# Attention score rows by way of DRAM lines, the last group graph by graph, and an urgent branch, in a four-layer graph network

## The chip, the cores and the metric

The kernel runs on one core of a Trainium2 chip. Its time is the device time of one execution in microseconds (us). Runs are compared by the median of several executions; one further execution was taken by the hardware profiler, and all views of the trace come from it. The engines are named as the profile names them: PE is TensorE (PEld its weight loads), DVE is VectorE, ACT is ScalarE, POOL is GpSimd, and SP is SyncE, which here issues DMAs. ACTq, DVEq and the like are the engines' own instruction queues. In the kernel's plan SP and ACTQ are the two queues for DMAs.

## What is computed

There are 128 graphs of 128 nodes with 256 features, and an adjacency matrix per graph. Four layers follow, each of the form x = x + f(relu(layernorm(x)), adj). All is float32.

```python
def _L0_gnn_ref(x, adj, weight, w_ih, w_hh, b_ih, b_hh):
    A = (adj != 0).astype(x.dtype)
    h = x
    for i in range(3):
        m = jnp.einsum('bnd,de->bne', h, weight[i])
        aggr = jnp.einsum('bst,bsd->btd', A, m)
        h = _gru_cell(aggr, h, w_ih, w_hh, b_ih, b_hh)
    return h

def _L1_gnn_ref(x, adj, relation, weight, bias):
    rel_ids = jnp.arange(1, weight.shape[0] + 1)
    masks = (relation[None] == rel_ids[:, None, None, None]).astype(x.dtype)
    h = jnp.einsum('rbnm,bmd->rbnd', masks, x)
    return jnp.einsum('rbnd,rdo->bno', h, weight) + bias

def _L2_gnn_ref(h, adj_mask, W, a):      # layer 3 is of the same kind
    Wh = jnp.einsum('bnd,od->bno', h, W)
    ei, ej = Wh @ a[:256], Wh @ a[256:]
    e = ei[:, :, None] + ej[:, None, :]
    e = jnp.where(e > 0, e, 0.2 * e)
    e = jnp.where(adj_mask == 0, -jnp.inf, e)
    alpha = jax.nn.softmax(e, axis=-1)
    return jnp.einsum('bij,bjo->bio', alpha, Wh)
```

For the change, the score matrix of the two attention layers matters: entry (i, j) is the sum of a number of node i, `ei`, and a number of node j, `ej`. With node i on the partitions, `ei` is a bias for each partition, but `ej` has to lie along the free axis, alike on all partitions. The first relational layer needs only one relation where the adjacency holds nothing but 0 and 1, as it does in these inputs; the kernel looks at the data to find that out.

## The kernel before, in words

The 128 graphs are handled in 32 groups of four (`G = 4`, `NG = 32`). For every group, `group(gi)` writes down operations: the loads (`load`, four DMAs on SP), a norm, three GRU steps (`step`, nearly all of the products, line 820), then the relational layer (`neighbours`), two attention layers (`attention` and `attend`) and the output (line 1096, on SP).

Nothing of the order is written by hand. Each operation is an `Op` with an engine, an estimated duration, and the buffers it reads and writes (whole or in parts). `Plan.order` then plays these durations through: it ranks each operation by the length of the way that hangs on it, moved by `PERIOD` (28 us) for each later group, and places again and again the operation that can start first; operations of up to `AHEAD = 4` groups mix. `LAG` and `HOP` are the allowances for a result to reach another engine (2500 ns for a DMA's landing), `OWN` for a result used on the same engine. The buffers (8 PSUM banks, 27 `big`, 10 `small`, 5 `xs` and others) are given out in this play too. The engines run the resulting lists strictly in order, with semaphores between them: an operation that has to wait on the chip holds everything behind it on its engine.

**The branch.** The operations up to the GRU steps are the same whatever the adjacency holds; later ones depend on it. The adjacency is therefore scanned: 32 loads on SP (line 508) and 32 maximum reductions on VectorE (L510), then one reduction (L513), a transpose on TensorE (L515), another reduction (L517) and a comparison into `found` (L519). All operations planned to start by then are issued; then all engines read `found` and branch (`values_load`, line 1111, and `tc.If`). In one side are all remaining operations with `neighbours`, in the other those with `relations`, which does not run here.

**Norm.** `norm` takes statistics for each graph (L532), then for each piece (a range of graphs) five small VectorE operations (L546 to L562) and a power on GpSimd (L558). Then ScalarE scales and shifts, two graphs in one operation (L574).

**Attention.** `attention(i, mask)` takes, for each graph, the sums for `ei` and `ej` (`terms`, L993) into columns of the tile `s`. `attend` then works on a piece. `rows` (L1018) transposes each column of `ej`, broadcast to 128 columns, on TensorE, so that a PSUM bank holds the row on all partitions. ScalarE adds `ei` as it copies the bank to the tile `e` (L1023). VectorE takes the leaky part (L1027), adds the mask and takes the minimum (L1030), ScalarE the exponential (L1036), VectorE the reciprocal (L1042, L1045). TensorE turns the weights round (L1054), they are evicted (L330, the line of all evictions that may run on ScalarE or VectorE), and for each pair of graphs come the weighted sum of nodes (L1065), an eviction, the product with the layer's weights (L1078) and the residual (L1088). In `neighbours`, L624 and L639 are the like products and L647 the residual.

A piece is the whole group (`whole`) for groups 0 to 28, and two graphs for the last three (`SPLIT = 3`).

Of the kernel before, what the change touches and what calls it, by code (L numbers as in the profile page):

```python
# [37 lines left out]
OWN = {"PE": 0, "ACT": 125, "DVE": 125, "POOL": 80, "SP": 0, "ACTQ": 0}  # L38
PERIOD = 28000
AHEAD = 4  # L40
SPLIT = 3
SPARE = (1, 0, 0, 3)
# [35 lines left out]
class Op:  # L78
    __slots__ = ("engs", "eng", "times", "ns", "fn", "deps", "heirs", "bufs", "group", "key", "port", "rank", "wait", "ready", "end")
# [12 lines left out]
class Plan:  # L92
# [6 lines left out]
    def op(self, eng, ns, fn, r=(), w=(), after=(), port=None):  # L99

        o = Op(*((eng, ns) if isinstance(eng, tuple) else ((eng,), (ns,))), fn, self.group)
        o.port = eng == "POOL" if port is None else port
        if self.shared:
            o.key = self.keys
            self.keys += 1
        deps = set(after)
        for items, writes in ((r, False), (w, True)):
            for item in items:  # L110
                buf, parts = item if isinstance(item, tuple) else (item, None)
                for other, wrote, theirs in buf.uses:
                    if buf.alone and o.engs + other.engs != ("PE", "PE"):
                        deps.add(other)
                    elif (writes or wrote) and other is not o:
                        if parts is None or theirs is None or parts & theirs:
                            deps.add(other)
                buf.uses.append((o, writes, parts))
                if buf not in o.bufs:
                    o.bufs.append(buf)  # L120
                    buf.left += 1
        o.deps = sorted(deps, key=lambda d: d.wait)
        o.wait = len(self.ops)
        for d in deps:
            d.heirs.append(o)
        self.ops.append(o)
        return o

    def order(self, pools, cut=None, prefix=()):
# [8 lines left out]
        for o in self.ops:  # L138
            o.rank = o.group * PERIOD - o.rank
            o.wait = len(o.deps)  # L140
# [112 lines left out]
def kernel(  # L253
# [40 lines left out]
    pools = [banks, xs, adjs, big, wide, half, small, mis]  # L294
# [3 lines left out]
    def build(general):  # L298
# [38 lines left out]
        def chunk(name):  # L337
            return Buf(big, name)
# [167 lines left out]
        for f in range(F):  # L506
# [7 lines left out]
            top.t[:, 0:1], most.t, AX.X, ALU.max), r=[most], w=[top])  # L514
        op("PE", 109, lambda: nc.tensor.transpose(pm.t[0:1, 0:P], top.t[:, 0:1], ident.t),  # L515
           r=[top, ident], w=[pm])
        op("DVE", 200, lambda: nc.vector.tensor_reduce(  # L517
            top.t[0:1, 1:2], pm.t[0:1, 0:P], AX.X, ALU.max), r=[pm], w=[top])
        verdict = op("DVE", 80, lambda: nc.vector.tensor_scalar(  # L519
            found, top.t[0:1, 1:2], 1.0, None, ALU.is_gt), r=[top])  # L520
# [5 lines left out]
        whole = (range(G),)  # L526

        def norm(xt, nm, pieces=whole):
# [39 lines left out]
            hs = []  # L568
            for g2 in range(G // 2):
                h = chunk(f"h{nm}{g2}")  # L570

                def scale(g2=g2, h=h):
                    for g in (2 * g2, 2 * g2 + 1):
                        nc.scalar.activation(  # L574
                            h.t[:, (g % 2) * D : (g % 2 + 1) * D], xt.t[:, g, :], AF.Relu,
# [3 lines left out]
                op("ACT", 2 * act(D, 2) + 85, scale,  # L579
                   r=[(xt, {2 * g2, 2 * g2 + 1}), (s, {(n, g) for n in ("rs", "mr") for g in (2 * g2, 2 * g2 + 1)})], w=[h])  # L580
                hs.append(h)
# [16 lines left out]
        def bias(xt):  # L598
            for g2 in range(G // 2):
                op("POOL", 1370, lambda g2=g2: nc.gpsimd.tensor_tensor(  # L600
                    xt.t[:, 2 * g2 : 2 * g2 + 2, :], xt.t[:, 2 * g2 : 2 * g2 + 2, :],
                    b1s.t.unsqueeze(1).to_broadcast([P, 2, D]), ALU.add),
                   r=[b1s], w=[(xt, {2 * g2, 2 * g2 + 1})])
# [7 lines left out]
        def neighbours(gi, xt, ai, aiT, m0, m3, late, pieces):  # L611
# [4 lines left out]
            hs, _ = norm(xt, f"1_{gi}", pieces)  # L616
            bias(xt)
            for g2 in range(G // 2):
                pr = bank(f"pr{gi}{g2}")

                def gather(g2=g2, pr=pr):
                    for g in range(2):
                        for k in range(KC):
                            nc.tensor.matmul(  # L624
                                pr.t[:, (2 * k + g) * P : (2 * k + g + 1) * P],
                                hs[g2].t[:, g * D + k * P : g * D + (k + 1) * P],
                                mT.t[:, (2 * g2 + g) * P : (2 * g2 + g + 1) * P],
                                start=True, stop=True,
                            )

                op("PE", 892, gather, r=[hs[g2], mT], w=[pr])
                hr = chunk(f"hr{gi}{g2}")
                evict(T, lambda hr=hr: hr.t, lambda pr=pr: pr.t, r=[pr], w=[hr])
                py = bank(f"py{gi}{g2}")

                def mix(hr=hr, py=py):
                    for g in range(2):
                        for k in range(KC):
                            nc.tensor.matmul(  # L639
                                py.t[:, g * D : (g + 1) * D],  # L640
                                hr.t[:, (2 * k + g) * P : (2 * k + g + 1) * P],
                                w1s.t[:, k, :],
                                start=(k == 0), stop=(k == KC - 1),
                            )

                op("PE", 2 * KC * 2 * D * PE_COL, mix, r=[hr, w1s], w=[py])
                op("DVE", dve(T), lambda g2=g2, py=py: nc.vector.tensor_tensor(  # L647
                    xt.t[:, 2 * g2 : 2 * g2 + 2, :], xt.t[:, 2 * g2 : 2 * g2 + 2, :],
                    py.t.rearrange("p (g d) -> p g d", g=2), ALU.add),
                   r=[py], w=[(xt, {2 * g2, 2 * g2 + 1})])  # L650

        def relations(gi, xt, ai, aiT, m0, m3, late, pieces):
# [55 lines left out]
        def group(gi):  # L708
# [272 lines left out]
            pieces = (range(2), range(2, G)) if gi >= NG - SPLIT else whole  # L981
            (relations if general else neighbours)(gi, xt, ai, aiT, m0, m3, late, pieces)
            unrelated(m2, m0, FAR, late)

            def attention(i, mask):
                hs, s = norm(xt, f"{2 + i}_{gi}", pieces)

                EI, EJ = 48, 52
                for g in range(G):
# [9 lines left out]
                    op("DVE", 690, terms, r=[hs[g // 2], ub[i]], w=[junk, (s, {("ei", g)})], port=True)  # L999
# [3 lines left out]
            def attend(i, mask, hs, s, gs, EI, EJ):  # L1003
# [9 lines left out]
                pe, e = bank(f"pe{nm}"), chunk(f"e{nm}")  # L1013
# [7 lines left out]
                op("PE", 110 * len(gs), rows, r=[ident, (s, {("ei", g) for g in gs})], w=[pe])  # L1021
                for g in gs:
                    op("ACT", 250, lambda g=g: nc.scalar.activation(  # L1023
                        at(e, g), at(pe, g), AF.Identity, bias=s.t[:, EI + g : EI + g + 1]),
                       r=[pe, (s, {("ei", g)})], w=[(e, {g})])
# [33 lines left out]
                for g2 in range(gs.start // 2, gs.stop // 2):  # L1059
                    pc, c, po = bank(f"pc{nm}{g2}"), chunk(f"cT{nm}{g2}"), bank(f"po{nm}{g2}")  # L1060

                    def weigh(g2=g2, pc=pc):
                        for g in range(2):
                            for k in range(KC):
                                nc.tensor.matmul(  # L1065
                                    pc.t[:, (2 * k + g) * P : (2 * k + g + 1) * P],
                                    hs[g2].t[:, g * D + k * P : g * D + (k + 1) * P],
                                    at(eT, 2 * g2 + g),
                                    start=True, stop=True,
                                )  # L1070

                    op("PE", 892, weigh, r=[hs[g2], eT], w=[pc])
                    evict(T, lambda c=c: c.t, lambda pc=pc: pc.t, r=[pc], w=[c])

                    def transform(c=c, po=po):
                        for g in range(2):
                            for k in range(KC):
                                nc.tensor.matmul(  # L1078
                                    po.t[:, g * D : (g + 1) * D],
                                    c.t[:, (2 * k + g) * P : (2 * k + g + 1) * P],  # L1080
                                    wa[i].t[:, k, :],
                                    start=(k == 0), stop=(k == KC - 1),
                                )

                    op("PE", 2 * KC * 2 * D * PE_COL, transform, r=[c, wa[i]], w=[po])
                    for g in range(2):
                        gg = 2 * g2 + g
                        op("DVE", 395, lambda g=g, gg=gg, po=po: nc.vector.scalar_tensor_tensor(  # L1088
                            xt.t[:, gg, :], po.t[:, g * D : (g + 1) * D], s.t[:, RI + gg : RI + gg + 1],
                            xt.t[:, gg, :], ALU.mult, ALU.add),  # L1090
                           r=[po, (s, {("rinv", gg)})], w=[(xt, {gg})])
# [69 lines left out]
```

## Time and profile before

| what | value |
|---|---|
| median of 3 runs | 2648.02 us (2647.67 to 2648.6) |
| the profiled execution | 2648.33 us |
| its span in the profile | 2646.5 us |
| TensorE transposes L1018 | 256, in sets of 4, 2 or 1 |
| ScalarE L1023, L1036 | 256 each, medians 373 and 394 ns |
| first start of the scan's loads, last of the scan's reductions | 21.3 us, 103.1 us |
| `found` written (L519) | 225.1 us |
| last residual L1088 begins to run | 2640.8 us |
| last output issued | 2641.7 us |
| granted TensorE clock, whole span | 0.994 |

The page lists busy times of the engines, the granted clock in slices of the span, and the chain of work that ended last, followed back from the last instruction. The other views are busy times by stretch, waits by releaser, and DMAs from issue to landing. Times within the trace count from the span's start.

### The profile page before, as it was taken

To read this page: it belongs to the slowest core of one execution; us is meant where nothing else is said; L and a number is where in the kernel's file an instruction comes from. 1 tells how busy PE (TensorE), PEld (TensorE's weight loads), DVE (VectorE), ACT (ScalarE), POOL (GpSimd) and SP (SyncE) were. 2 spreads that over 40 slices of the span, in tenths; PEclk is the share of its full clock that TensorE was granted. 3 is DMA by queue.
4 is the path that set the end of the run, shared out by engine and by line. 5 is a ranking of instruction groups with operands and counts; after the bars stand their busy time and mean duration, and the time that the engine had idled before them with its cause. 6 is when DMAs were issued, how large, how long until landed. Compare 5 with 4: busy or idle time off the path is not lost.

```text
span 2646.5 us, 40354 instructions
## 1 busy us (share of the span) xinstructions
PE 2606.2 (98%) x14041; PEld 2321.0 (88%) x14041; DVE 2204.8 (83%) x6376; ACT 1566.5 (59%) x3792; POOL 466.0 (18%) x400
## 2 busy tenths in 40 slices
PE   8999999999999999999999999999999999999995
PEld 7888888888888888988898988888888889888884
DVE  8868898888888888888888888888888888888885
ACT  5446666656566565565565656565656655665553
POOL 1112122111121111121111111111111111211121
PEclk9999999999999999999999999999999999999997
DMA  6100000000000000000000000000000000000000
GB/s 208 42 1 1 29 21 25 25 25 25 10 16 25 25 25 25 1 25 25 25 25 25 1 25 25 25 25 21 5 25 25 25 25 2 24 25 25 9 9 18
DMA packets 77494, 65.22 MB, mean 25 GB/s; under 512 B 3936, under 2 KB 73184, under 8 KB 77280
## 3 DMA queue, kind: packets, MB, share of 16 engines
q1 hardware_dynamic: 76192, 61.50, 7.8%
q8 instruction: 112, 1.84, 0.3%
q10 hardware_dynamic: 1088, 1.05, 0.1%
q14 instruction: 102, 0.84, 0.1%
HBM read 45.75 MB, written 16.78 MB: 24 GB/s over the span
## 4 chain that ended last, share of the span: by engine, by line
PE 94%; DVE 4%; ACT 1%; issue 0%; DMA 0%; POOL 0%; ACTq 0%; DVEq 0%
PE bank L820 64%; PE bank L1078 8%; PE bank L1065 4%; PE bank L762 4%; PE bank L639 4%; PE bank L954 3%; PE bank L733 2%; PE bank L624 2%; PE bank L1054 1%; PE bank L1018 1%; DVE junk L993 0%; PE bank L445 0%; DVE small L532 0%; DVE big L922 0%; DVE big L942 0%
## 5 line engine op out<-in xcount | busy, mean ns | idle before, releaser
L330 ACT COPY big<-bank 128x512 f32<-128x512 f32 (+1 forms) x978 | 455.5, 481 | 496.7 <-PE bank L820 426.3
L820 PE MATMUL bank<-big,rz_h 128*128 128x256 f32 x1536 | 462.8, 383 | 0.3
L820 PE MATMUL bank<-big,rz_a 128*128 128x256 f32 x1536 | 456.8, 379 | 0.0
L929 POOL TENSOR_TENSOR big<-wide,big 128x512 f32<-128x512 f32 x192 | 245.6, 1298 | 1108.7 <-ACT big L927 951.6
L820 PE MATMUL bank<-wide,rz_h 128*128 128x256 f32 x1152 | 342.9, 379 | 0.3 <-DVE wide L330 0.3
L820 PE MATMUL bank<-wide,rz_a 128*128 128x256 f32 x1152 | 342.6, 379 | 0.0
L820 PEld LDWEIGHTS bank<-big,rz_a 128*128 128x128 f32 x1536 | 291.8, 190 | 39.8
L820 PEld LDWEIGHTS bank<-big,rz_h 128*128 128x128 f32 x1536 | 279.7, 190 | 47.3 <-ACT big L330 15.0
L558 POOL TENSOR_TENSOR small<-small,nhalf 128x4 f32<-128x4 f32 (+1 forms) x137 | 138.8, 1014 | 970.4 <-DVE small L556 951.6
L574 ACT ACTIVATE big<-xs,small 128x256 f32<-128x256 f32 x512 | 269.8, 592 | 48.4 <-DVE small L562 48.0
L837 ACT ACTIVATE big<-big,b_rz 128x256 f32<-128x256 f32 x576 | 258.2, 499 | 44.3 <-DVE big L843 42.1
L330 DVE COPY big<-bank 128x512 f32<-128x512 f32 (+1 forms) x276 | 159.9, 581 | 143.8 <-PE bank L820 89.3
L927 ACT ACTIVATE big<-big,bih_s 128x512 f32<-128x512 f32 x192 | 128.7, 715 | 205.4 <-DVE big L912 109.1
L820 PEld LDWEIGHTS bank<-wide,rz_a 128*128 128x128 f32 x1152 | 218.9, 190 | 29.7
L820 PEld LDWEIGHTS bank<-wide,rz_h 128*128 128x128 f32 x1152 | 216.3, 190 | 28.5 <-DVE wide L330 0.5
L1078 PE MATMUL bank<-wa,big 128*128 128x256 f32 x1024 | 235.5, 383 | 2.6 <-ACT big L330 2.6
L843 DVE TENSOR_TENSOR big<-bank,big 128x512 f32<-128x512 f32 x288 | 196.2, 686 | 47.3 <-PE bank L820 46.8
L820 PE MATMUL bank<-big,n_h 128*128 128x256 f32 x768 | 228.2, 380 | 0.8 <-DVE big L330 0.7
L1078 PEld LDWEIGHTS bank<-wa,big 128*128 128x128 f32 x1024 | 195.0, 191 | 30.6 <-ACT big L330 4.2
L820 PE MATMUL bank<-big,n_a 128*128 128x256 f32 x768 | 217.9, 379 | 0.0
L912 DVE TENSOR_TENSOR big<-bank,big 128x256 f32<-128x256 f32 x384 | 160.6, 419 | 61.6 <-PE bank L820 57.9
L993 DVE CUSTOM_DVE_ANT_0 junk<-big,ub 128x256 f32<-128x256 f32 x512 | 192.6, 421 | 1.6 <-ACT big L574 1.5
(91 smaller groups left out, 4723.0 us busy)
## 6 DMA issues: line engine op xcount, KB each, us to landing
xs<-in_x_dram SPq DMA_DIRECT2D x64, 256.0 KB, 4.0
out_dram<-xs SPq DMA_DIRECT2D x29, 512.0 KB, 3.3
adjs<-in_adj_dram SPq DMA_DIRECT2D x32, 256.0 KB, 4.3
adjs<-in_adjT_dram SPq DMA_DIRECT2D x32, 256.0 KB, 4.5
big<-in_adj_dram SPq DMA_DIRECT2D x32, 256.0 KB, 3.0
out_dram<-xs SPq DMA_DIRECT2D x6, 256.0 KB, 2.2
big<-in_wihT_dram ACTq DMA_DIRECT2D x3, 256.0 KB, 6.4
big<-in_whhT_dram SPq DMA_DIRECT2D x3, 256.0 KB, 5.8
```

The costliest lines, as they stand in the source:

```text
L330: (nc.scalar.copy if eng == "ACT" else nc.vector.tensor_copy)(dst(), src())
L558: op("POOL", 1130, lambda: nc.gpsimd.tensor_tensor(columns(RS), columns(RS), nhalf.t[:, gs.start : gs.stop], ALU.pow), r=[nhalf], w=[own(" ...
L574: nc.scalar.activation(h.t[:, (g % 2) * D : (g % 2 + 1) * D], xt.t[:, g, :], AF.Relu, bias=s.t[:, MR + g : MR + g + 1], scale=s.t[:, RS + ...
L639: nc.tensor.matmul(py.t[:, g * D : (g + 1) * D], hr.t[:, (2 * k + g) * P : (2 * k + g + 1) * P], w1s.t[:, k, :], start=(k == 0), stop=(k = ...
L820: nc.tensor.matmul(ps.t[:, m * W : (m + 1) * W], a.t[(slice(None), *row, j, slice(m * P, (m + 1) * P))], b[j](), start=(start and m == x = ...
L837: op("ACT", act(W, 1) + 40, lambda m=m, c=c: nc.scalar.activation(t[c].t[:, g2 * W : (g2 + 1) * W], src.t[:, m * W : (m + 1) * W], AF.Tanh ...
L843: op("DVE", dve(T), lambda: nc.vector.tensor_tensor(c.t, ps.t, c.t, ALU.add), r=[ps], w=[c])
L912: op("DVE", dve(W), lambda: nc.vector.tensor_tensor(dst(), ps.t[:, :W], dst(), ALU.add), r=[ps], w=[((ws if more else vs)[c], {g2})])
L927: op("ACT", act(T, 1) + 85, lambda nn=nn, c=c: nc.scalar.activation(nn.t, vs[c].t, AF.Tanh, bias=bi.t[:, 4 + c : 5 + c]), r=[vs[c], bi], w ...
L929: op("POOL", 1230, lambda qq=qq, nn=nn, c=c: nc.gpsimd.tensor_tensor(qq.t, hT.t[:, c, :], nn.t, ALU.subtract), r=[(hT, {(c, 0), (c, 1)}), ...
L993: nc.vector.tensor_tensor_reduce(out=junk.t[:, v * D : (v + 1) * D], in0=part, in1=ub[i].t[:, v, :], op0=ALU.mult, op1=ALU.add, scale=1.0, ...
L1078: nc.tensor.matmul(po.t[:, g * D : (g + 1) * D], c.t[:, (2 * k + g) * P : (2 * k + g + 1) * P], wa[i].t[:, k, :], start=(k == 0), stop=(k ...
```

## The change

Five things are changed.

1. In `attend`, where the piece is the whole group (`len(gs) == G`), the transposes are left out. SP stores the four `ej` columns of `s` into a DRAM tile `line` (four graphs by 128 nodes), then loads this line into `e` on all partitions. ScalarE's addition reads `e` and writes `e`. There are four such lines, given out by the planner. Smaller pieces keep the transposes.
2. For the last group (`SINGLE = 1`), pieces and pairs become single graphs (`singly`): the norm, the bias, the products and the evictions each take one graph. `product`, `sums` and `mix` now hold the products for `neighbours` and `attend` both; for pairs they issue the same matmuls as before. Parts of `h` are tracked for each graph.
3. The operations L513 to L519 get `rush=RUSH` (60 us), which is taken off their rank, so that they are placed ahead of others. The 32 loads and 32 reductions of the scan do not get it.
4. `OWN` for SP and ACTQ goes from 0 to 2500 ns: a DMA that needs an earlier one's result on the same queue is planned that much later.
5. Some planned durations are written per graph (the scaling, the bias).

```diff
-OWN = {"PE": 0, "ACT": 125, "DVE": 125, "POOL": 80, "SP": 0, "ACTQ": 0}
+OWN = {"PE": 0, "ACT": 125, "DVE": 125, "POOL": 80, "SP": 2500, "ACTQ": 2500}
+SINGLE = 1
+RUSH = 60000
...
-            o.rank = o.group * PERIOD - o.rank
+            o.rank = o.group * PERIOD - o.rank - o.rush
...
+    dram = ctx.enter_context(tc.tile_pool(name="dram", bufs=1, space=bass.MemoryType.DRAM))
+    lines = [dram.tile([G, P], F32, name=f"line_{j}") for j in range(4)]
+    pools = [banks, xs, adjs, big, wide, half, small, mis, lines]
...
-            top.t[:, 0:1], most.t, AX.X, ALU.max), r=[most], w=[top])
+            top.t[:, 0:1], most.t, AX.X, ALU.max), r=[most], w=[top], rush=RUSH)
...
+        whole, pairs, singly = (
+            tuple(range(g, g + n) for g in range(0, G, n)) for n in (G, 2, 1))
...
-                op("ACT", 2 * act(D, 2) + 85, scale,
-                   r=[(xt, {2 * g2, 2 * g2 + 1}), (s, {(n, g) for n in ("rs", "mr") for g in (2 * g2, 2 * g2 + 1)})], w=[h])
+                op("ACT", len(gs) * (act(D, 2) + 43), scale,
+                   r=[(xt, set(gs)), (s, {(n, g) for n in ("rs", "mr") for g in gs})],
+                   w=[(hs[gs.start // 2], set(gs))])
...
+        def product(gs, nm, hs, r, weight, w):
+
+            N = len(gs) * D
+            pc, c, po = bank(f"pc{nm}"), chunk(f"c{nm}"), bank(f"po{nm}")
+            op("PE", 446 * len(gs), lambda: sums(gs, pc, hs, weight),
+               r=[(hs[gs.start // 2], set(gs)), r], w=[pc])
+            evict(N, lambda: c.t[:, :N], lambda: pc.t[:, :N], r=[pc], w=[c])
+            op("PE", len(gs) * KC * 2 * D * PE_COL, lambda: mix(gs, po, c, w), r=[c, w], w=[po])
+            return po
...
-            pieces = (range(2), range(2, G)) if gi >= NG - SPLIT else whole
-            (relations if general else neighbours)(gi, xt, ai, aiT, m0, m3, late, pieces)
+            pieces = singly if gi >= NG - SINGLE else pairs if gi >= NG - SPLIT else whole
+            duos = singly if gi >= NG - SINGLE else pairs
+            (relations if general else neighbours)(gi, xt, ai, aiT, m0, m3, late, pieces, duos)
...
-                op("PE", 110 * len(gs), rows, r=[ident, (s, {("ei", g) for g in gs})], w=[pe])
+                terms = (s, {("ei", g) for g in gs})
+                if len(gs) == G:
+
+                    line, pe = Buf(lines, f"line{nm}"), e
+                    op("SP", 400, lambda: nc.sync.dma_start(
+                        out=line.t.rearrange("g p -> p g"), in_=columns(EJ)), r=[terms], w=[line])
+                    op("SP", 1280, lambda: nc.sync.dma_start(
+                        out=e.t, in_=line.t.rearrange("g p -> (g p)").partition_broadcast(P)),
+                       r=[line], w=[e])
+                else:
+                    pe = bank(f"pe{nm}")
+                    op("PE", 110 * len(gs), rows, r=[ident, terms], w=[pe])
                 for g in gs:
                     op("ACT", 250, lambda g=g: nc.scalar.activation(
                         at(e, g), at(pe, g), AF.Identity, bias=s.t[:, EI + g : EI + g + 1]),
-                       r=[pe, (s, {("ei", g)})], w=[(e, {g})])
+                       r=[(pe, {g}), (s, {("ei", g)})], w=[(e, {g})])
```

## The prediction

> **What bounds the kernel now.** First the page's head, its busy times, and the chain of work that ended last.
>
> ```profile
> span 2646.5 us, 40354 instructions
> PE 2606.2 (98%) x14041; PEld 2321.0 (88%) x14041; DVE 2204.8 (83%) x6376; ACT 1566.5 (59%) x3792; POOL 466.0 (18%) x400
> PE 94%; DVE 4%; ACT 1%; issue 0%; DMA 0%; POOL 0%; ACTq 0%; DVEq 0%
> ```
>
> 94% of the chain is TensorE itself, so work taken off TensorE should shorten the kernel one for one, wherever TensorE never waits. The busy times of stretches say where that is (columns: stretch, length, then busy time and instructions of PE, PEld, DVE, ACT, POOL, then the granted clock, DMA share and GB/s).
>
> ```profile
> 448.19:528.37 80.18, 80.18 (x438) 71.80 (x437) 67.25 (x195) 48.99 (x120) 14.84 (x12) 1.00 0.07 21
> 20.00:2580.00 2560.00, 2556.10 (x13835) 2281.85 (x13833) 2161.95 (x6185) 1530.96 (x3695) 455.50 (x382) 1.00 0.08 23
> 2580.00:2641.70 61.70, 38.36 (x160) 29.37 (x160) 34.35 (x165) 25.76 (x70) 8.77 (x11) 0.75 0.04 14
> ```
>
> Between 20 and 2580 us TensorE idles 2560 - 2556.1 = 3.9 us in all: a group of four graphs costs 80.18 us of pure TensorE. After 2580 it is another program: TensorE is busy 38.4 of 61.7 us at 0.75 of its clock, VectorE 34.35 of 61.7 (56%), and neither is full. There the latency of one group decides. So the kernel has two limits, and the change touches both.
>
> **Row transposes of whole groups (TensorE).** The chain inside one steady group has these two steps.
>
> ```profile
> 457.75 0.44 PE bank L1018 x4
> 489.84 0.44 PE bank L1018 x4
> ```
>
> These are the four row transposes of each attention layer, 0.44 us for four. Removed for groups 0 to 28, two layers each: 29 x 2 x 0.44 = 25.5 us. TensorE has no idle time there to absorb it, so I count all 25.5. At the other end, nothing is gained if TensorE waits for the replacement instead; that is the third rival. The freed PSUM bank I count as nothing: with 3.9 us idle there is hardly a wait it could end.
>
> **What replaces them.** Per layer: a store from SP (four columns of `s` to a line in DRAM, 512 runs of 4 bytes), then a load that waits for it (2 KB copied to each of 128 partitions), then L1023 reading `e` instead of a bank. The trace has no such pair; the nearest rows, in us from issue to landing:
>
> ```profile
> adjs<-in_adj_dram SPq DMA_DIRECT2D x32, 256.0 KB, 4.3
> out_dram<-xs SPq DMA_DIRECT2D x6, 256.0 KB, 2.2
> big<-in_adj_dram SPq DMA_DIRECT2D x32, 256.0 KB, 3.0
> bih_s<-in_bih_dram SPq DMA_DIRECT2D x1, 3.0 KB, 4.7
> ```
>
> For the store: 2.2 (a store, large runs) to 4.7 (small runs, in the opening rush of loads). Nearest by number of runs is the adjacency load, 128 x 4 = 512, so 4.3. For the load: the scan's loads have the same 128 runs of 2 KB, 3.0, between 2.6 and 5.5 in their own list. Together 7.3 us, ends 4.8 and 10.2. The plan allows 400 + 2500 + 100 + 1280 + 2500 + 40 ns = 6.8 us, so `e` is 0.5 us later than the plan thinks (ends: 2.0 early, 3.4 late). L1023 then stands in ScalarE's order, and behind it the evictions L330 that free PSUM banks. What covers it is in the waits from 448 to 1200 us, 9.4 groups (who waited for whom: us, times, longest):
>
> ```profile
> ACT big L330 <- PE bank L820: 127.0, 95, 3.6
> ```
>
> ScalarE stands 13.5 us per group waiting for TensorE at evictions, against 2 x 0.5 = 1.0 late. Cost taken: 0. Without the cover it is 58 x 0.5 = 29 us, and 58 x 3.4 = 197 at the far end.
>
> On one steady group this adds to SP four issues of about 0.4 us. SP is in order, and stands for most of a period at an output (29 waits, 2057.4 us, up to 77.3):
>
> ```profile
> SPq L1096 <- DVE xs L1088: 2057.4, 29, 77.3
> SPq L1111 <- DVE found L519: 144.3, 1, 144.3
> ```
>
> The lines must therefore be placed ahead of the output, and when the load waits for its store, a group's four loads queue behind it for some 4.3 us. The loads issued at 404.6 to 407.2 us landed about 4 us later and were first read at 415.3 (L532), with the adjacency at 418.0: margins near 6 us and 7 us. 0. L1023's source moves to SBUF: the nearest SBUF form, L1036, has a median of 394 ns against 373, so 232 x 21 ns = 4.9 us of ScalarE, under the same cover. Buffers: `e` is held some 7 us longer, twice per 80 us, 0.2 of 27 `big` buffers. 0.
>
> A rule against this part stands in the Trainium skill, "DMA: Bandwidth & Descriptors", Rules for kernel authors: an access pattern without contiguous runs becomes one descriptor per element and should be rearranged. The trace has no run of 4 bytes; its 24-byte rows took 4.7 us and the 512-byte rows 4.3 us, which show latency and no such cliff. [...]
>
> **Urgent verdict.** Four small operations after the 32 scan reductions. The last reduction starts at 103.1 us, L513 at 104.1, but the transpose L515 only at 224.0 and `found` at 225.1; SP stands 144.3 us for it. Urgent, the branch comes near 107 us. TensorE lost nothing at the branch (busy 80.00 of 80 from 200 to 280 us), and from 100 to 108 us it is busy 8.00 of 8, so moving it saves nothing. Bounds: plus 3 us if TensorE runs dry there once (the plan's allowance for a branch), minus 3.9 if the earlier mix removes every idle moment. Taken: 0.
>
> **Last group graph by graph.** Its GRU ends with L944 near 2583.5; its last residual at 2641.7. Today two halves alternate, and a half's layer repeats every 18.6 us (L647 at 2604.6, L1088 at 2621.8 and 2640.8). Note what the halves cost in the tail's chain:
>
> ```profile
> 2632.26 3.78 PE bank L1078 x8
> 2638.79 2.01 PE bank L1078 x8
> ```
>
> Eight products of the same kind take 2.01 or 3.78 us, so part of the latency is clock. VectorE's work is 34.35 us, plus small operations: two more norm pieces x 3 norms x 5 x about 0.075 us pitch = 2.3, so 36.7. At its present share (56%) that is 36.7 / 0.56 = 65.5, a loss of 3.8. At the whole kernel's 83% it is 44.2, a gain of 17.5. For one graph I add up a chain of about 9 us per attention layer from these rows (statistics 0.4, moments 0.6, power 1.0, scale 0.6, terms 0.8, rows to weights 3.3, weigh and mix with evictions 2.0, residual 0.5); four graphs' VectorE work per layer is about 10.8. So the layer repeats between 10.8 and 18.6; midway, 14.7, saves about 4 per attention layer, and half as much in the first: 10. Taken: 10, which is VectorE at 71%.
>
> The skill's "TensorE: Matmul & The Clock Gate", Part 1, says the clock halves after an idle window of about 3.4 us. The 0.75 above fits; by it shorter gaps between graphs would save a further 2 us or so, an estimate left out of the sum.
>
> **Sum.** 2648.33 (span 2646.5 and 1.8 around it) - 25.5 - 10 - 0 = 2612.8. The profiled execution is 0.3 above the median of 2648.02: **2612.5**.
>
> The order is planned anew, and waits may reappear. The worst steady stretch, 2360 to 2440 us, has TensorE 78.67 of 80, 1.33 idle; 29 such groups would give back 38.6.
>
> **Rivals.**
> - *Rows only*: the tail's halves already overlap, and VectorE keeps its 56%. For it: four times as many power operations of 0.7 us each, in order on POOL. Against it: VectorE is under half busy after 2622 us. 2648.0 - 25.5 = 2622.5, up to 2626 with the loss of 3.8.
> - *Partly given back*: the new order has idle moments, half of the 38.6: 2612.5 + 19 = 2632. For it: stretches with pieces already show 1.3 us. Against it: the steady groups show none.
> - *Landings hold ScalarE* (slower): every load lands later than planned, L1023 blocks the evictions behind it, TensorE runs out of banks and waits. It decides once TensorE loses (25.5 + 10) / 58 = 0.61 us at each of 58 places. At 1.2 us it costs 70: 2682. For it: 512 tiny runs are in no row, and plan and landing agree only to some us. Against it: the 13.5 us per group that ScalarE waits today.
> - *It doesn't do what it says*: the 232 transposes vanish only where a piece is the whole group; the diff has that for exactly groups 0 to 28. The early branch does happen but is worth 0, which is in the forecast.
>
> **Chances.** Forecast 0.57, rows only 0.18, partly given back 0.09, landings 0.13, gains and waits cancelling within 0.2% 0.03. 0.2% (5.3 us) is about what can be told from no change here, the three runs lying within 0.9 us. So faster 0.84, same 0.03, slower 0.13. The likeliest's own range: 2612.5 - 7.5 - 3 = 2602 to 2622. To leave out no more than 2 in 10 it reaches to the partly given back: 2600 to 2634.
>
> **What would show it.** L1018 with 24 transposes left; the steady period 80.18 - 0.88 = 79.3 us; TensorE still idle under 8 us from 20 to 2580; the two line transfers together 5 to 8 us; `found` near 106 us; the stretch from the last L944 to the last L1088 at about 48 us instead of 58, with VectorE near 70%. I am wrong if ScalarE shows long waits for a DMA at L1023 and TensorE waits for L330 in steady groups, or if VectorE stays at 56% in the tail.

## The result and the profile after

The changed kernel takes 2949.67 us (median of 4; 2948.87 to 2952.65) beside 2647.85 us: a ratio of 1.1142, 95% interval 1.1122 to 1.1161. It is 302 us slower where 35 us were forecast as gained. The page's head after, with the row of the score's addition (L1045, which was L1023) that now reads the line:

```profile
span 2948.4 us, 40366 instructions
PE 2677.7 (91%) x13809; PEld 2352.8 (80%) x13809; DVE 2204.4 (75%) x6528; ACT 1547.1 (52%) x3698; POOL 480.4 (16%) x408
L1045 ACT ACTIVATE big<-big,small 128x128 f32<-128x128 f32 x232 | 79.7, 392 | 326.3 <-DMA big<-line 326.3
```

The 232 transposes are gone (14041 to 13809 matmuls), and yet TensorE is busy for longer and has become 91%. ScalarE stood 326.3 us at L1045 for the load of the line. The landings of the two new DMAs, in us from issue:

```profile
big<-line SPq DMA_DIRECT2D x58, 256.0 KB, 4.9
line<-small SPq DMA_DIRECT2D x58, 2.0 KB, 10.2
```

The store takes 10.2 us (8.9 to 12.8), not 4.3; the load 4.9, not 3.0. Together that is 15.1 where the plan allows 6.8. The waits, who for whom:

```profile
SPq L1038 <- DMA line<-small: 532.7, 54, 13.0
ACT big L1045 <- DMA big<-line: 326.3, 53, 13.6
PE bank L830 <- ACT big L336: 194.4, 39, 12.5
```

This is a chain of three queues. SP stands for the store, ScalarE stands for the load, and TensorE stands for the evictions (L336, before L330) that are queued behind L1045 on ScalarE. SP's own timeline (start, length, line) shows what the landing alone doesn't:

```profile
1043.64 0.37 SPq L1036 DMA_DIRECT2D line<-small  x1
1055.37 0.34 SPq L1038 DMA_DIRECT2D big<-line  x1
1055.80 0.39 SPq L1036 DMA_DIRECT2D line<-small  x1
1066.10 0.33 SPq L1038 DMA_DIRECT2D big<-line  x1
```

Two attention layers come together, of one group and of another. The second store stands in SP's order behind the first load, and that load is issued 11.7 us after the first store. So the second load is issued more than 22 us after the first store. This place is worse than most: over the 28 such pairs the second store follows the first by 9.6 us in the median. In e4 below, where every engine's order is the same and the store is short, it is 9.0 us. So the landings themselves make most of the delay, and SP's queue adds to it. The outputs of two neighbouring groups leave some 90 us apart (1004.65 and 1094.81 us; 88.9 in the median) instead of 80.2.

Busy times up to the last transposes of the last GRU update, and from there to the last residual (columns as in the prediction):

```profile
20.00:2901.60 2881.60, 2637.99 (x13648) 2321.80 (x13647) 2165.45 (x6327) 1520.19 (x3620) 468.84 (x384) 0.95 0.11 26
2901.60:2943.90 42.30, 28.33 (x115) 21.47 (x113) 30.22 (x173) 17.11 (x50) 9.75 (x16) 0.76 0.06 19
```

The same two stretches of the kernel before:

```profile
20.00:2584.90 2564.90, 2557.92 (x13842) 2283.26 (x13841) 2166.69 (x6204) 1535.29 (x3704) 457.54 (x384) 1.00 0.08 23
2584.90:2641.70 56.80, 36.55 (x154) 27.96 (x153) 29.60 (x146) 21.43 (x62) 6.74 (x8) 0.76 0.05 15
```

Before the last GRU's end TensorE idles 243.6 us instead of 7.0, and its busy time grew by 80 us with less work at a granted clock of 0.95 instead of 1.00. Only the tail is shorter, 42.3 for 56.8 us.

### The profile page after: what moved, and what is told of

Same layout as the page of the kernel before. It is cut to its first block, busy times and chain, and to the rows that moved or that the text cites. A ratio compares the mean times of both kernels' runs of the same rounds, so it can differ in the third digit from the quotient of the medians.

```text
span 2948.4 us, 40366 instructions
## 1 busy us (share of the span) xinstructions
PE 2677.7 (91%) x13809; PEld 2352.8 (80%) x13809; DVE 2204.4 (75%) x6528; ACT 1547.1 (52%) x3698; POOL 480.4 (16%) x408
## 5 line engine op out<-in xcount | busy, mean ns | idle before, releaser
L336 ACT COPY big<-bank 128x512 f32<-128x512 f32 (+2 forms) x936 | 441.5, 490 | 481.8 <-PE bank L830 345.0
L830 PE MATMUL bank<-big,n_a 128*128 128x256 f32 x768 | 231.9, 405 | 180.8 <-ACT big L336 170.3
L830 PE MATMUL bank<-wide,rz_h 128*128 128x256 f32 x1152 | 369.7, 405 | 8.2 <-ACT wide L336 7.9
L830 PE MATMUL bank<-wide,rz_a 128*128 128x256 f32 x1152 | 365.6, 401 | 0.0
L830 PEld LDWEIGHTS bank<-big,n_a 128*128 128x128 f32 x768 | 138.8, 200 | 203.0 <-ACT big L336 180.8
L567 POOL TENSOR_TENSOR small<-small,nhalf 128x4 f32<-128x4 f32 (+2 forms) x143 | 148.8, 1041 | 882.3 <-DVE small L565 865.8
L830 PEld LDWEIGHTS bank<-wide,rz_h 128*128 128x128 f32 x1152 | 236.4, 206 | 46.2 <-ACT wide L336 8.3
L830 PEld LDWEIGHTS bank<-wide,rz_a 128*128 128x128 f32 x1152 | 234.9, 204 | 36.9
L336 DVE COPY big<-bank 128x512 f32<-128x512 f32 (+2 forms) x328 | 173.3, 530 | 108.0 <-PE bank L830 91.2
L1045 ACT ACTIVATE big<-big,small 128x128 f32<-128x128 f32 x232 | 79.7, 392 | 326.3 <-DMA big<-line 326.3
L830 PE MATMUL bank<-big,n_h 128*128 128x256 f32 x768 | 232.2, 385 | 11.7 <-ACT big L336 11.3
## 6 DMA issues: line engine op xcount, KB each, us to landing
line<-small SPq DMA_DIRECT2D x58, 2.0 KB, 10.2
```

The lines of the kernel that those rows point to most:

```text
L336: (nc.scalar.copy if eng == "ACT" else nc.vector.tensor_copy)(dst(), src())
L567: op("POOL", 1130, lambda: nc.gpsimd.tensor_tensor(columns(RS), columns(RS), nhalf.t[:, gs.start : gs.stop], ALU.pow), r=[nhalf], w=[own(" ...
L830: nc.tensor.matmul(ps.t[:, m * W : (m + 1) * W], a.t[(slice(None), *row, j, slice(m * P, (m + 1) * P))], b[j](), start=(start and m == x = ...
L1045: op("ACT", 250, lambda g=g: nc.scalar.activation(at(e, g), at(pe, g), AF.Identity, bias=s.t[:, EI + g : EI + g + 1]), r=[(pe, {g}), (s, { ...
```

## The experiments

Times are medians, each beside the kernel before on the same chip (2646.99 to 2647.49 us). A run of bytes is a stretch that lies side by side in DRAM. The parts of the change that only alter the plan (items 4 and 5) are in all twelve; none tries them by themselves.

| run | rows of groups 0 to 28 | branch | last group | us | ratio to before, interval |
|---|---|---|---|---|---|
| e1_no_lines | transposes | urgent | single | 2646.90 | 0.9999 (0.9990 to 1.0009) |
| e6_rush_only | transposes | urgent | pairs | 2644.31 | 0.9989 (0.9979 to 0.9998) |
| e7_single_only | transposes | as before | single | 2654.85 | 1.0026 (1.0016 to 1.0036) |
| e2_only_lines | line, 512 runs | as before | pairs | 2934.55 | 1.1092 (1.1073 to 1.1110) |
| e3_plan_told | line, 512 runs | urgent | single | 2697.36 | 1.0192 (1.0175 to 1.0209) |
| e8_columns | line, 4 x 128 runs | urgent | single | 2840.62 | 1.0738 (1.0720 to 1.0756) |
| e4_runs16 | line, 128 runs, numbers interchanged | urgent | single | 2627.07 | 0.9925 (0.9908 to 0.9941) |
| e5_fix | line, 128 runs | urgent | single | 2626.38 | 0.9920 (0.9903 to 0.9936) |
| e9_columns_apart | line, 4 x 128 runs, 16 bytes apart | urgent | single | 2626.21 | one execution, no interval |
| e10_fix_pairs | line, 128 runs | urgent | pairs | 2623.25 | 0.9909 (0.9894 to 0.9924) |
| e11_fix_alone | line, 128 runs | as before | pairs | 2659.39 | 1.0046 (1.0033 to 1.0060) |
| e12_fix_told | line, 128 runs | urgent | pairs | 2639.68 | 0.9971 (0.9961 to 0.9982) |

### Which part loses

e1 takes the lines away from the changed kernel, e2 leaves only them.

```diff
# e1_no_lines
-                if len(gs) == G:
+                if len(gs) > G:
# e2_only_lines
-SINGLE = 1
+SINGLE = 0
-RUSH = 60000
+RUSH = 0
```

> The changed kernel with the row transposes kept in every group (no DRAM lines); urgent branch and the last group graph by graph stay. Theory (the two line transfers make the whole loss): the steady period is back at 80.2 us, TensorE is idle under 8 us from 20 us to the last group, and only the shorter tail is left of the change (57.1 to 43.7 us from the last GRU update to the last residual in the two traces), so 2648 - 13 = 2635, between 2628 and 2642. Rival (the new order with the urgent branch or the finer pieces loses time as well): 2655 or more.

> The changed kernel with no urgent branch (RUSH = 0) and the last group in pairs as before (SINGLE = 0); the DRAM lines stay. Theory: the loss is all the lines', and the tail's 13 us come back as well: 2950 + 13 = 2963, between 2945 and 2985, ScalarE waiting 300 to 360 us for the line's load. Rival (the early branch brings attention work into the start of the run, where the plan is worse): under 2920.

Without the lines nothing of the loss is left (2646.90), and with only the lines it is nearly whole (2934.55). The lines make the loss. But e1 did not gain its 13 us either, and e2 was faster than the changed kernel by 15 us where 13 slower was expected; both times lie outside the ranges of the theory and of the rival. So the other two parts do not do what I took them to do; e6, e7, e10 and e11 return to that.

### Is it the landing, and why is it so long?

e4 changes one access pattern. Each partition's four numbers go to DRAM side by side. The load then brings them in another order, so e4's scores are wrong; it is there for its times.

```diff
# e4_runs16
-                        out=line.t.rearrange("g p -> p g"), in_=columns(EJ)), r=[terms], w=[line])
+                        out=line.t.rearrange("g p -> (g p)").rearrange("(p g) -> p g", g=G), in_=columns(EJ)), r=[terms], w=[line])
```

> The changed kernel, with the store writing each partition's four numbers next to each other: 128 runs of 16 bytes in place of 512 runs of 4 bytes. The load reads the same 2 KB, so the row scores of nodes and graphs of the group are interchanged: the four groups of numbers are not where the attention looks for them. Theory (the number of tiny runs makes the store slow): the store lands in 2.5 to 4.5 us instead of 10.2, the pair is near the plan's 6.8 us, ScalarE waits under 80 us for it, and the time is 2610 to 2660. Rival (it is the write to DRAM and its receipt that take 10 us, whatever the runs): store 8 us or more, time over 2900.

The store lands in 1.4 us, and 323 us are gone. The landings and the busy times of e4, to set beside those of the changed kernel above:

```profile
big<-line SPq DMA_DIRECT2D x58, 256.0 KB, 3.9
line<-small SPq DMA_DIRECT2D x58, 2.0 KB, 1.4
```

```profile
20.00:2577.60 2557.60, 2542.15 (x13648) 2268.19 (x13647) 2179.32 (x6327) 1526.79 (x3620) 468.83 (x384) 1.00 0.11 29
```

All engines' instructions stand in the same order in both kernels; only the store's form differs. So this is the late landing by itself. It breaks the loss in two: TensorE's idle time is 15.5 us instead of 243.6, and the same 13648 matmuls are busy for 2542 us at clock 1.00 instead of 2638 at 0.95. Of 324 us, 228 were waits and 96 were matmuls at the lower clock after the waits. Matmul by matmul, nine tenths of the extra time falls on those that start within 7 us after a wait of more than 2 us. Right after one such wait, from 1058.5 to 1068.5 us, the granted clock is 0.50. That agrees with the Trainium skill, "TensorE: Matmul & The Clock Gate", Part 1, by which idle windows of a few us lower the clock: the waits here were up to 12.5 us.

e3 leaves the store as it is and tells the plan how long it takes.

```diff
# e3_plan_told
-                    op("SP", 400, lambda: nc.sync.dma_start(
+                    op("SP", 7700, lambda: nc.sync.dma_start(
-                    op("SP", 1280, lambda: nc.sync.dma_start(
+                    op("SP", 2400, lambda: nc.sync.dma_start(
```

> The changed kernel, with the plan told what the transfers measured: the store planned at 7700 + 2500 ns (10.2 us landed) in place of 400 + 2500, the load at 2400 + 2500 ns (4.9 us) in place of 1280 + 2500. Nothing else changes but the order this gives. Theory (the loss is that in-order engines stand for results that the plan believes to be there): ScalarE's wait for the line falls from 326 us to under 60, TensorE is saturated again at 79.3 us per group, and the time is 2648 - 25.5 - 13 = 2610, between 2603 and 2640. Rival (15 us per layer are too long for four groups in flight, or SP's queue is the limit): over 2690, TensorE waiting in the plan itself.

The store's landing and the busy times up to the last GRU update's transposes:

```profile
line<-small SPq DMA_DIRECT2D x58, 2.0 KB, 8.4
20.00:2647.60 2627.60, 2577.87 (x13649) 2267.31 (x13648) 2205.62 (x6403) 1494.70 (x3545) 452.99 (x384) 0.99 0.10 28
```

The first half came as the theory had it. ScalarE no longer waits for the line at all, and 252 of the 302 us are back, with a store that is still slow (8.4 us). So most of the loss came from an order written for a transfer of another length. But 2697 is far from the 2603 to 2640 expected and inside the rival's range, over 2690. Against the same stretch of e4 TensorE idles 34 us longer (49.7 instead of 15.5) and its matmuls take 36 us more. Its waits are not for the line, and the outputs leave every 81.0 us, not 79.3. Which of the rival's two reasons holds e3 there, or another, stays open.

e8 and e9 ask what makes the store slow. Both write one column at a time, 128 runs of 4 bytes per DMA. In e8 the runs lie side by side in 512 bytes; in e9 they are 16 bytes apart, as the line ordered by node has them. e9 loads and reads this line as e5 below does; only its store is shown.

```diff
# e8_columns
-                    op("SP", 400, lambda: nc.sync.dma_start(
-                        out=line.t.rearrange("g p -> p g"), in_=columns(EJ)), r=[terms], w=[line])
+                    for g in gs:
+                        op("SP", 400, lambda g=g: nc.sync.dma_start(
+                            out=line.t[g : g + 1, :].rearrange("g p -> p g"),
+                            in_=s.t[:, EJ + g : EJ + g + 1]), r=[terms], w=[(line, {g})])
# e9_columns_apart
+                            out=line.t.rearrange("g p -> (g p)").rearrange("(p g) -> p g", g=G)[:, g : g + 1],
```

> The changed kernel with the store cut into four DMAs, one for each graph's column: 128 runs of 4 bytes each, which go to 512 bytes that lie together; same result. Theory (each 4-byte run costs its DMA engine about 8.8 us / 24 further runs = 0.37 us, wherever it goes): the four land one after the other, the last about 10 us or more after the first issue, and the time stays over 2900. Rival (it is the stride of 512 bytes between one partition's four numbers that is slow): each lands in 2 to 3 us, the last within 5 us, and the time falls under 2750.

> The kernel with the line ordered by node, its store cut into four DMAs, one for each graph: 128 runs of 4 bytes again, now 16 bytes apart in DRAM. In the earlier store of single columns 128 runs of 4 bytes, lying side by side in 512 bytes, took 8.5 us; 128 runs of 16 bytes side by side took 1.4. Theory A (a 4-byte run to DRAM is slow in itself, wherever it lies): 7 us or more per store, time over 2750. Theory B (several engines write into one small stretch of DRAM at once; a column of 512 bytes gives each of the 16 engines 32 bytes, here it is 128): 1.4 to 3 us per store, time under 2660.

The landings of single columns, e8:

```profile
line<-small SPq DMA_DIRECT2D x232, 0.5 KB, 8.5
```

and e9:

```profile
line<-small SPq DMA_DIRECT2D x232, 0.5 KB, 2.3
```

e8 is a miss for both of its sides: 2840.62 us lies between their ranges. A DMA with a quarter of the runs takes 8.5 us instead of 10.2, and 7.5 at the least, so the stride of 512 bytes between a partition's numbers isn't needed for a slow store. Four such DMAs can be in flight at once, so e8 alone doesn't clear the number of runs; e9 does. It has as many runs of the same 4 bytes in as many DMAs, and each store takes 2.3 us (1.4 at the least), as its theory B had it. What differs is how closely a DMA's runs lie in DRAM. The packets themselves are not slow: for the 11 stores of the changed kernel that no other transfer of such runs overlaps, the records of its packets (the pieces that the DMA engines move) end 1.3 us after the issue, and the store lands after 8.9 to 10.9 us. The likely reason, argued and not shown, is that several DMA engines rewrite the same small stretch of DRAM in turn. The Trainium skill, "DMA: Bandwidth & Descriptors", Specifications, says that transfers under 512 bytes are done by reading and rewriting, which would fit; e9 and e4 show that a store of such runs need not be slow.

### The whole computation with the short store

e5 keeps e4's store and reads the numbers from where they are: the load goes into a tile of its own, and ScalarE reads every fourth number.

```diff
# e5_fix
-                    line, pe = Buf(lines, f"line{nm}"), e
+                    line, pe = Buf(lines, f"line{nm}"), chunk(f"raw{nm}")
...
-                        out=e.t, in_=line.t.rearrange("g p -> (g p)").partition_broadcast(P)),
+                        out=pe.t, in_=line.t.rearrange("g p -> (g p)").partition_broadcast(P)),
...
+                    return pe.t.rearrange("p (n g) -> p g n", g=G)[:, g, :] if len(gs) == G else at(pe, g)
...
-                        at(e, g), at(pe, g), AF.Identity, bias=s.t[:, EI + g : EI + g + 1]),
+                        at(e, g), row(g), AF.Identity, bias=s.t[:, EI + g : EI + g + 1]),
```

> The whole computation again, with the short store: each partition writes its four numbers as one run of 16 bytes, the load brings the line, still ordered by node, into a tile of its own, and ScalarE's addition reads every fourth number of it. One more big buffer is held for a few us per layer, nothing else differs from the changed kernel. Theory (the store's 512 runs were the loss): the store lands in about 1.4 us, ScalarE does not wait for the line, and the time is that of the kernel with interchanged numbers, 2627, between 2618 and 2634, below the kernel before. Rival (the further buffer, or reading at a step of 16 bytes, costs ScalarE as much): over 2642, L1050 well above 400 ns each.

2626.38 us: 21 us below the kernel before, and no more than e4. The group of the addition in e5 (busy us, mean ns of one, then idle before it and for whom):

```profile
L1049 ACT ACTIVATE big<-big,small 128x128 f32<-128x128 f32 x232 | 108.8, 520 | 0.6 <-DMA big<-line 0.6
```

Reading at a step of 16 bytes makes one addition 520 ns instead of 392 (the row of L1045 above), 30 us of ScalarE in all, and the time does not show it. ScalarE's room covers a longer instruction; it did not cover a late one.

### The branch and the last group

```diff
# e6_rush_only (on e1)
-SINGLE = 1
+SINGLE = 0
# e7_single_only (on e1)
-RUSH = 60000
+RUSH = 0
```

> Of the change only the urgent branch (RUSH) and the planned durations: no DRAM lines, the last group in pairs. Theory A (the branch costs or gains nothing, since TensorE is saturated on both sides of it; the finer pieces give back themselves what they gain): 2647, within 4. Theory B (the early branch hides a gain of the finer pieces by losing as much): 2652 to 2660.

> Of the change only the last group graph by graph (SINGLE = 1) and the planned durations: no DRAM lines, no urgency. Theory A (the shorter chain of the last group makes the plan do group 30's work before the last GRU instead of beside the tail; TensorE's idle time in the tail falls by 6 us and rises by 4 ahead of it): 2643 to 2648. Theory B (the urgent branch took the gain away): 2633 to 2640.

e6 lies in theory A's range (2643 to 2651), but the branch is not worth nothing: urgent, with the planned durations, it gains 3.2 us. e7 lies outside both ranges: the single graphs lose 7.4. The two don't add up. With the urgency, single graphs cost 2.6 us (e1 against e6). Where they lose shows in the same two stretches of e7:

```profile
20.00:2605.40 2585.40, 2570.28 (x13880) 2292.91 (x13879) 2182.62 (x6252) 1530.89 (x3695) 455.14 (x384) 1.00 0.08 23
2605.40:2649.20 43.80, 29.73 (x115) 23.17 (x112) 30.19 (x173) 17.03 (x50) 9.76 (x16) 0.73 0.05 18
```

The tail is 13 us shorter, as expected. But the last GRU ends 20.5 us later. There are 115 matmuls in the tail instead of 154: the work of group 30 that filled TensorE beside the tail is now done ahead of it. TensorE's idle time in the tail falls from 20.3 to 14.1 us, and ahead of it rises from 7.0 to 15.1. That is 1.9 us more in all. The larger part is elsewhere: nearly the same number of matmuls (13995 and 13996) keeps TensorE busy for 2600.0 us instead of 2594.5, 5.5 longer, and the granted clock in the tail is 0.73 instead of 0.76. A shorter way to the end makes the last group less urgent in the plan; that this is the reason follows from how the ranks are made, and was not tried by itself.

```diff
# e10_fix_pairs (on e5)
-SINGLE = 1
+SINGLE = 0
# e11_fix_alone (on e10)
-RUSH = 60000
+RUSH = 0
# e12_fix_told (on e10)
-                    op("ACT", 250, lambda g=g: nc.scalar.activation(
+                    op("ACT", 470 if len(gs) == G else 250, lambda g=g: nc.scalar.activation(
```

> The kernel with the 16-byte runs in the right order, with the last group in pairs as in the kernel before (SINGLE = 0); urgent branch kept. Theory (the last group graph by graph costs 3 to 7 us whatever the rows do: without the lines it took 2646.9 with the urgency against 2644.3 in pairs, and 2654.9 against 2647.5 without the urgency): 2618 to 2624. Rival (with the lines its shorter tail does pay): 2627 or more.

> Only the lines with 16-byte runs in the right order: no urgent branch, last group in pairs. Theory (the urgent branch is worth about 3 us by itself): 3 us above the kernel with pairs and urgency, 2621 to 2628. Rival (it matters only through the order that happens to come out): within 1 us of it or below.

> The kernel with pairs and urgency, with the plan told that the addition from the line takes 470 ns of ScalarE (its busy time divided by its count) in place of 250. Theory (ScalarE has room, the plan's error is absorbed): within 3 us of the kernel with pairs and urgency. Rival (the plan's error leaves TensorE waiting): 5 us or more below it.

e10 is the fastest of all, 2623.25 us (24.0 below before): the last group in pairs is worth 3 us here too. e11 is a large miss. With the short store but the late branch, the kernel is slower than before, and the urgency is worth 36 us instead of 3. The stretch after the branch in e11 and in e10:

```profile
240.00:400.00 160.00, 138.51 (x704) 120.77 (x703) 123.84 (x410) 92.60 (x216) 33.85 (x29) 0.91 0.11 29
```

```profile
240.00:400.00 160.00, 160.00 (x865) 143.44 (x864) 135.30 (x401) 98.86 (x233) 29.72 (x24) 1.00 0.10 27
```

In e11 TensorE idles 21.5 us there at a clock of 0.91 and does 704 matmuls instead of 865. The kernel before has its branch late as well (`found` at 225.1 us, in e11 at 247.6) and idles 0.6 us in the same stretch; there the rows came from TensorE in half a microsecond. So with the short store the two parts of the change belong together. ScalarE waits only 2.6 us for the line in all of e11, so the loss lies in the order that the plan makes and not in late landings; what in that order loses is not shown. No run tries the urgency by itself with the slow store. e12 misses on the other side: an addition planned at its measured length makes the kernel 16 us slower than e10, and its outputs leave every 80.1 us instead of 79.2. So the order that comes out of the plan is by itself worth as much as most gains here, and a truer number does not always make a better one.

## Why the prediction was wrong

**What bounds the kernel** held. In e10, where ScalarE waits 0.7 us in all for the line, TensorE is never idle from 1000 to 2000 us.

**Row transposes, 25.5 us**: right in size. e10 and e6 differ by the lines and the order that follows from them. TensorE's busy time falls by 26.9 us (2603.1 to 2576.2), and the outputs of e10 leave every 79.21 us instead of 80.18, near the 79.3 predicted. The time falls by less, 2644.31 - 2623.25 = 21.1 us: the groups at the end give some of it back in idle time (11.1 us instead of 6.4 before the last GRU's end). How much is left depends on the order too, in e12 7.6 us; that the order came out well in e10 was luck.

**What replaces them** is the step that failed: "Nearest by number of runs is the adjacency load, 128 x 4 = 512, so 4.3". Its ends, 2.2 to 4.7, left out the 10.2 us measured. All my rows were loads, or stores of long runs; none was a store of scattered numbers into a small stretch of DRAM, and e8 and e9 show that the count of runs, by which I chose the row, isn't what sets the time. For the load I took 3.0 where 4.9 came, inside the ends given. So `e` came 8.3 us later than the plan thought, not 0.5. (The plan's 6.8 us is 6.72: the 100 ns are not counted between two DMAs of one queue.)

**The cover** failed too: "Cost taken: 0", because ScalarE stood 13.5 us per group waiting for TensorE. Most of those waits are still there (345.0 us in all for the same evictions and releaser, 426.3 before). But of the 8.3 us of lateness at each of 58 places ScalarE stood 5.6 on average at L1045. An in-order ScalarE that stops at L1045 holds evictions that TensorE needs then, and gets nothing for the time it could wait later. And **SP**: I counted the group's loads that queue behind the first load, "0", and not the other layer's store. That one left 0.6 us later in the median pair than in e4; its share of the loss was not separated.

**The third rival** had the mechanism and the place right, and its size wrong: 1.2 us per place where (2949.67 - 2612.5) / 58 = 5.8 were missed against the forecast. It also had no term for the clock, 96 of the 324 us between e4 and the changed kernel. I gave it 0.13 from a far end of 10.2 us for the whole pair; the pair took 15.1.

**Urgent verdict, 0**: `found` came at 115.2 us, later than the 107 I reckoned. Without the other parts (e6) it gains 3.2 us, near my bound of 3.9 and not 0; with the short lines it is worth 36 (e11), for which the prediction had no term.

**Last group, 10 us**: the latency fell by 14.5 us, within the 17.5 I allowed. The gain didn't follow: e1 gains nothing and e7 loses 7.4 us. I priced the length of the tail, not TensorE's idle time in it. Other work that fills the tail has to be done at another time. With the idle time as the measure, the most to be had was 20.3 us, of which the finer pieces saved 6, gave back 8 ahead and lost 5.5 in longer matmuls (e7).

## What to carry to other kernels

A transfer that replaces work on the busy engine has to be measured by itself in its exact access pattern before an order is planned around it: here the same 2 KB took 1.4 or 10.2 us, by where the runs lie in DRAM. In a planned order with in-order queues, an engine's spare time in total says little about whether it covers a late operation: here 8.3 us of lateness at each of 58 places cost 5.6 us (324 / 58), with 13.5 us of waits per group to spare. Price a tail by the idle time of the bound engine in it, not by its length.

## What the runs showed of the hardware

- 128 runs of 4 bytes from SBUF to DRAM landed in 8.5 us when they lay side by side in 512 bytes (e8), and in 2.3 us at a distance of 16 bytes (e9), in both with up to four such stores in flight; 128 runs of 16 bytes side by side took 1.4 us (e4), and 512 runs of 4 bytes in 2 KB 10.2 us (the changed kernel).
- ScalarE's addition read float32 at a step of 16 bytes in 520 ns for 128 x 128 (e5), against 392 ns without a step (the changed kernel).
- Waits of up to 12.5 us on TensorE cost 96 us more in slower matmuls, at a mean granted clock of 0.95, beside 228 us of waiting (the changed kernel against e4).
